# Handing out row gathers by a queue, and taking one more row block of a sparse product over edge lists

## The chip, the cores and the metric

The kernel runs on one NeuronCore of a Trainium2 chip. The metric is the device time of one execution in microseconds, and its median over runs. The engines are called by the names that the profile uses: PE (matrix products) with PEld (its weight loads), DVE (VectorE), ACT (ScalarE), POOL (GpSimd, which also issues the indirect gathers) and SP (which issues the big loads).

## The reference, cut to what matters

Four graph layers share one sparse 4096 x 4096 matrix `adj`; each is a residual with a layer norm. The change lies in layer 1, which multiplies by `adj` three times:

```python
def cheb_conv(x, L, W, b):
    Tx0 = x
    out = Tx0 @ W[0]
    Tx1 = L @ x
    out = out + Tx1 @ W[1]
    for k in range(2, W.shape[0]):
        Tx2 = 2.0 * (L @ Tx1) - Tx0
        out = out + Tx2 @ W[k]
        Tx0, Tx1 = (Tx1, Tx2)
    return out + b
h = elu(cheb_conv(x, adj, W0, b0))     # 128 -> 256
h = elu(cheb_conv(h, adj, W1, b1))     # 256 -> 128
x = layernorm(x + h)
```

The kernel does `adj @ x` (product 1, giving `t1`), `adj @ t1` (product 2, giving `t2` and from it `h` and `v`), and then, with the second convolution factored, `adj @ v` (product 3, giving `w`) and `adj @ w` (product 4). `adj` is sparse: the kernel provides for up to 24 entries in a row apart from the diagonal. All four products are in float32.

## The kernel before, in words

**Dense products.** `propagate` (lines 723 to 737) walks over row blocks of 512 rows. For each it loads eight chunks of 512 x 512 (1 MB each, through SP, into a pool `ld` of five buffers) and does four 128x512 matrix products for each chunk. A float32 product of 128x512 shows as two records in the profile, so that a row block is 64 records. After each chunk a hook is called (`seen`); the text counts these hooks from 0 in each product, eight to a row block. Product 1 runs over the row blocks 2, 3, 0, 4, 5, 1, 6, 7, that is 64 hooks; its chunk order is `finished`, the order in which layer 0 ended its blocks, which works out as 0, 7, 5, 1, 6, 2, 3, 4. Product 2 is dense in six row blocks (48 hooks), product 3 in five.

**Edge lists.** While chunks pass by, `Lists.take` (line 1392) finds the entries of each row on DVE: for each of a chunk's four 128-row tiles one MAX8 (line 1402) and one FIND_INDEX8 (line 1403). "A take" below is one chunk: four such pairs. Where the chunk holds the diagonal, ACT first copies each tile into a single buffer `copied` (line 1399) and DVE clears the diagonal (line 1401). `Lists.build` (line 1411) turns what was found into a list for a row block, in three parts. The lists of row blocks 0, 1, 2 (`PAIRED`) also need the matrix entries in both directions; these come by 36 gathers for each block (`pairs`, line 1533, landing in `both_ways`) and are unpacked by `paired` (line 1540).

**Sparse products.** With its list known, a row block needs no chunk. For each tile of 128 rows (a "unit") POOL gathers nine times 128 rows of the vector's table in DRAM (`rows_of`, line 1549), `weigh` (line 1554) does three TENSOR_SCALAR and six SCALAR_TENSOR_TENSOR on DVE, and `product` does one 128x128 product with the identity and three with the gathered rows. The tables are written block by block by `store` (line 1564). Product 2 takes row blocks 0 and 1 in this way (eight units, `second_product`, line 1605), product 3 row blocks 0 to 2 (twelve units, `third_product`, line 1672). In product 1 all eight row blocks are dense.

**What orders the work.** The order on PE and ACT is set by a scheduler when the program is built. On DVE, what goes through `chained` (line 1385) keeps the order in which it is written; in products 2 and 3 the takes, builds and weighs are chained, while in product 1 nothing is, and the scheduler mixes takes with other work there. POOL keeps program order. Each gather is one instruction on POOL (`by_index`, line 1523) followed by `pause` (line 1567), a 128x1 multiply of a constant with itself. Gathers are written in bursts: nine for a unit, or all 36 of a list, at one hook. In product 1 the 36 gathers for list 0 are written nine at a time, once in a row block, each time behind a pause that reads a column of the last finished `t1` block (line 765).

```python
def by_index(self, out, of, index):
    tc.keep_in_program_order(nc.gpsimd.indirect_dma_start(out, None, of, bass.IndirectOffsetOnAxis(ap=index, axis=0)))
    tc.keep_in_program_order(self.pause())
```

**After layer 1's third product** `sparse_layers` (line 1734) does product 4, six dense row blocks with two sparse ones, and then layers 2 and 3 over the lists.

Of the kernel before, what the change touches and what calls it, by code (L numbers as in the profile page):

```python
# [11 lines left out]
F32 = mybir.dt.float32  # L12
# [9 lines left out]
P = 128  # L22
# [18 lines left out]
LAST = [0, 1]  # L41
FAR = [4, 5, 6, 7]
EARLY = 7
NONE = -1e30
# [3 lines left out]
def adj_resnorm_d4(ctx: ExitStack, tc: tile.TileContext, x_in, xT_in, adj, adjT, pairs, diag_in, w0g, w0gT, a0, w1a, b1a,  # L48
# [633 lines left out]
    def network(usual):  # L682

        with ExitStack() as whole:
# [3 lines left out]
            with ExitStack() as first, ExitStack() as l1h_pool:  # L688
# [66 lines left out]

                made = lists.build(0) if usual else None
                done = []

                def beside_first(ib, n, c, a):
                    if 0 < c < FAR[0] or ib in LAST and c in FAR:  # L760
                        lists.take(ib, c, a)
                    if (len(done), n) in ((1, 0), (1, 4), (2, 0)):
                        next(made)
                    if len(done) > 2 and n == 3:
                        tc.keep_in_program_order(lists.pause(t1[:, done[-1] * TB, 0:1]))
                        fetch(0, TB * 9 // 4)

                for ib, blk, p in propagate(lambda jt: x[:, jt, :], finished, seen=beside_first, blocks=[2, 3, 0, 4, 5, 1, 6, 7]):
                    nc.scalar.copy(t1T[:, blk], p)
                    q = transpose4(ps_tr, "ptr", lambda k: t1T[:, (ib * TB + k) * P:(ib * TB + k + 1) * P])  # L770
                    nc.vector.tensor_copy(t1[:, ib * TB:(ib + 1) * TB, :], q)
                    done.append(ib)
                    if usual:
                        lists.store(2, ib, t1)

                v = state.tile([P, NT, F], F32, name="v")
# [4 lines left out]
                def second_end(ib, t2T):  # L781
# [11 lines left out]
                    nc.scalar.copy(v[:, ib * TB:(ib + 1) * TB, :], q)  # L793
                    done[-1] = ib
                    if usual:
                        lists.store(0, ib, v)

                second = second_product(lists, l1w, pairs, t1, t1T, xT, hT, v, done, t2_of, second_end) if usual else None

# [12 lines left out]
                if usual:  # L812
                    fetch(PAIRED[-1], TB * 9)
                    lists.paired(PAIRED[-1])
                    l1s = l1h_pool.enter_context(tc.tile_pool(name="l1s", bufs=2, reuse_waits="tile"))
                    third = third_product(lists, l1s, ps_tr, ps_mm, v, w, hT, W1B, wd, h0T)
# [5 lines left out]
                for ib, blk, p in propagate(lambda jt: v[:, jt, :], beside=times_w1, seen=third, blocks=[b for b in range(NB) if not usual or b not in PAIRED]):  # L822
# [4 lines left out]
                    if usual:  # L827
                        lists.chained(r)
                        lists.store(1, ib, w)
                    ph = ps_mm.tile([P, IB], F32, name="pmm")  # L830
# [489 lines left out]
    class Lists:  # L1320
# [3 lines left out]
        def __init__(self, whole, first, layer, own_entries):  # L1324
# [5 lines left out]
            self.table_early = dram.tile([N + 1, F + H], F32, name="table_early")  # L1330
            self.tables = [dram.tile([N + 1, F], F32, name=f"rows{n}") for n in range(3)]
            self.spread = dram.tile([NB, P, TB * SLOTS], BF16, name="spread")
            self.top = state.tile([P, NT, NB, 8], F32, name="top", tag="dv")
            self.at = keep.tile([P, NT - TB, NB, 8], U16, name="at")
            self.diag = own_entries
            self.last = None
            nc.scalar.dma_start(self.diag, diag_in)
            self.source = keep.tile([P, NT, NEAR + QT], I32, name="source")
# [184 lines left out]
        def by_index(self, out, of, index):  # L1523
            tc.keep_in_program_order(nc.gpsimd.indirect_dma_start(out, None, of, bass.IndirectOffsetOnAxis(ap=index, axis=0)))  # L1524
            tc.keep_in_program_order(self.pause())

# [77 lines left out]

    def second_product(lists, pool, pairs, t1, t1T, xT, hT, v, done, t2_of, second_end):
        units = len(LAST) * TB
# [15 lines left out]

        def pull(u):
            deque(lists.rows_of(u, got[u], 2), 0)

        def weigh(u):
            here = pool.tile([P, F], F32, name="here2", bufs=1)
            lists.weigh(u, t1[:, tile_of(u), :], got[u], here, got[u][:, E:E + QT, :], True)
            made[u] = here

        def product(u):
            t, k = tile_of(u), u % TB
            if k == 0:
                sums[0] = pool.tile([P, IB], F32, name="t2T")
            p = lists.psum.tile([P, P], F32, name="u")
            nc.tensor.matmul(p, made.pop(u), ident, start=True, stop=False)
            for j in range(QT):
                nc.tensor.matmul(p, got[u][:, j, :], got[u][:, E + j, :], start=False, stop=j == QT - 1)
            t2_of(sums[0][:, k * P:(k + 1) * P], p, slice(t * P, (t + 1) * P))
            if k == TB - 1:  # L1640
                second_end(PAIRED[u // TB], sums.pop(0))

        for c, h in ((1, 0), (2, 14)):
            build = lists.build(c, True)
            for n in range(3):
                at(h + 3 * n, next, build)
        at(0, pull, 0)
        at(0, pull, 1)
        at(7, fetch, 1, TB * E)
        at(8, lists.paired, 0)  # L1650
        at(26, lists.paired, 1)
        for u, h in enumerate((9, 11, 27, 30, 33, 35, 41, 44)):
            at(h, weigh, u)
            at(h + 1, product, u)
        for u, h in ((2, 12), (3, 13), (4, 25), (5, 25), (6, 35), (7, 37)):
            at(h, pull, u)
        at(26, fetch, 2, 12)
        at(45, fetch, 2, TB * E)
        hooks = [0]

        def seen(ib, n, c, a):
            h = hooks[0]
            hooks[0] += 1
            if c in FAR:
                lists.take(ib, c, a, True)
            for f in plan.pop(h, ()):
                f()
            if h == 47:
                assert not plan and not made and not sums
        return seen  # L1670

    def third_product(lists, pool, ps_tr, ps_mm, v, w, hT, W1B, wd, h0T):
        units = len(PAIRED) * TB
        E = NEAR + QT
        got, made = {}, {}

        def pull(u):
            if u < units:
                got[u] = pool.tile([P, E, F], F32, name="got3", bufs=3)
                deque(lists.rows_of(u, got[u], 0), 0)  # L1680

        def weigh(u):
            here = pool.tile([P, F], F32, name="here3")
            hot = pool.tile([P, QT, P], F32, name="hot3")
# [3 lines left out]
        def product(u):  # L1688
# [8 lines left out]
            nc.vector.tensor_tensor(w[:, t, :], p, here, ALU.add)  # L1697
            pull(u + 2)
            if u % TB == TB - 1:
# [12 lines left out]

        build = builds()
        pull(0)
        pull(1)
        plan = {}
        for u, h in enumerate((6, 9, 11, 14, 16, 19, 22, 24, 27, 30, 32, 35)):
            plan.setdefault(h, []).append(lambda u=u: weigh(u))
            plan.setdefault(h + 1, []).append(lambda u=u: product(u))
        plan[36].append(lambda: (deque(lists.values(3), 0), deque(lists.values(4), 0)))  # L1720
        hooks = [0]

        def seen(ib, n, c, a):
# [4 lines left out]
            for f in plan.pop(h, ()):  # L1728
                f()
            if h == 39:  # L1730
                assert not plan and next(build, None) is None
        return seen

    def sparse_layers(enter, lists, w, h0T):
# [274 lines left out]
        with tc.manual_schedule(engines={mybir.EngineType.PE, mybir.EngineType.DVE, mybir.EngineType.Activation,  # L2009
# [51 lines left out]
            for u, h in enumerate((7, 10, 13, 16, 19, 22, 25, 28)):  # L2061
                plan.setdefault(h, []).append(lambda u=u: weigh(u))
                plan.setdefault(h + 1, []).append(lambda u=u: product(u))
            pulls = pull()
            known = None
# [122 lines left out]
```

## Time and profile before

| what | value |
|---|---|
| median of 11 runs | 1644.76 us (1640.62 to 1654.07) |
| the profiled execution | 1647.62 us, span 1645.8 us |
| product 1 (335.4 to 562.8 us of the span) | PE busy 227.0 of 227.4, DVE 198.2, POOL 44.0 |
| product 2 (562.8 to 800) | PE busy 229.3 of 237.2, DVE 197.3, POOL 173.6 |
| product 3 (800 to 1000) | PE busy 188.8 of 200, DVE 160.1, POOL 149.6 |
| clock granted to PE from 335 to 1000 us | 1.00 |

The span is what the profiler saw of the program; the execution's own time has 1.8 us around it. The stages are cut where PE's first product of each kind begins. A busy time is the union of the records of an engine's instructions in the stretch.

### The profile page before, as it was taken

How to read it: one execution, taken by the hardware profiler on the slowest of the kernel's cores; microseconds unless marked ns; L12 is line 12 of the kernel's file. 1: busy time of each engine (PE TensorE's matmuls, PEld its weight loads, DVE VectorE, ACT ScalarE, POOL GpSimd, SP SyncE). 2: the span in 40 equal slices, each digit the busy share in tenths (PEclk: the TensorE clock that was granted, in tenths of full speed). 3: DMA queues.
4: the chain of work that ended last, by engine and by line, in shares of the span. 5: the costliest groups of instructions: out<-in, count | busy, mean ns of one | idle time of the engine just before them, and what ended most of it. 6: DMA issues, size and time to landing. Idle time of an engine off the chain costs nothing.

```text
span 1645.8 us, 16500 instructions
## 1 busy us (share of the span) xinstructions
PE 1473.4 (90%) x4740; PEld 712.4 (43%) x4744; DVE 1140.1 (69%) x3209; ACT 387.9 (24%) x698; POOL 837.0 (51%) x1336
## 2 busy tenths in 40 slices
PE   6899999999999999999999999799925798879885
PEld 3344444544444444454444454444413344444444
DVE  5887655789887897988699950355426855666776
ACT  5775540010000011121200000123213111122234
POOL 0000000000242088848486888888686688888841
PEclk9899999999999999999999999899967788889998
DMA  9867776479798886867587888799865577678773
GB/s 381 338 257 301 255 259 239 177 260 326 300 329 308 308 283 210 292 203 274 176 296 250 288 285 291 239 311 285 285 160 149 176 237 246 225 229 291 233 191 101
DMA packets 111199, 421.47 MB, mean 256 GB/s; under 512 B 21685, under 2 KB 48314, under 8 KB 71290
## 3 DMA queue, kind: packets, MB, share of 16 engines
q1 hardware_dynamic: 59984, 360.01, 60.8%
q0 software_dynamic: 22656, 36.17, 9.0%
q10 hardware_dynamic: 28458, 24.14, 5.0%
q8 instruction: 39, 0.64, 0.2%
q14 instruction: 62, 0.51, 0.1%
HBM read 404.39 MB, written 15.86 MB: 255 GB/s over the span
## 4 chain that ended last, share of the span: by engine, by line
PE 47%; DVE 25%; POOL 12%; DMA 8%; issue 5%; ACT 2%; DVEq 0%; ACTq 0%; POOLq 0%
PE pacc L731 16%; PE pacc L424 12%; PE pp L2076 6%; POOL got L1846 5%; DMA got<-table,source 4%; PE pp L1957 3%; DVE at L1403 3%; DVE top L1402 3%; POOL got L1524 2%; POOL idle L1569 2%; DMA got<-rows,source 2%; DVE gw L1882 1%; DVE here L1562 1%; DVE acc L1970 1%; POOL value L1524 1%
## 5 line engine op out<-in xcount | busy, mean ns | idle before, releaser
L1846 POOL DMA_INDIRECT got<-table,source x267 | 255.5, 957 | 64.8 <-issue 58.8
L1957 PE MATMUL pp<-chunk,xT 128*128 128x512 f32 x496 | 244.4, 634 | 1.2 <-ACT xT L1928 0.7
L731 PE MATMUL pacc<-chunk,x 128*128 128x512 f32 x512 | 222.7, 593 | 0.0
L1524 POOL DMA_INDIRECT got<-rows,source x180 | 183.5, 1020 | 67.4 <-issue 37.0
L424 PE MATMUL pacc<-chunk,hw 128*128 128x512 f32 x408 | 189.2, 608 | 0.8 <-DVE hw L467 0.7
L1360 POOL IOTA i<- 128x384 int32 (+3 forms) x4 | 0.9, 237 | 346.6 <-PE pden L412 329.5
L2076 PE MATMUL pp<-chunk,w 128*128 128x512 f32 x384 | 173.0, 600 | 0.0
L731 PE MATMUL pacc<-chunk,t 128*128 128x512 f32 x384 | 170.3, 593 | 0.0
L731 PEld LDWEIGHTS pacc<-chunk,x 128*128 128x128 f32 x512 | 96.1, 190 | 114.6 <-issue 114.6
L731 PE MATMUL pacc<-chunk,v 128*128 128x512 f32 x320 | 144.5, 597 | 0.0
L1402 DVE MAX8 top<-chunk 128x8 f32<-128x512 f32 x196 | 128.5, 677 | 11.8 <-DMA chunk<-in_adjT 11.8
L1957 PEld LDWEIGHTS pp<-chunk,xT 128*128 128x128 f32 x496 | 94.3, 203 | 91.3 <-issue 85.5
L1403 DVE FIND_INDEX8 at<-top,chunk 128x8 uint16<-128x512 f32 x196 | 133.1, 684 | 0.0
L1569 POOL TENSOR_TENSOR idle<-idle 128x1 f32<-128x1 f32 x508 | 114.2, 225 | 8.8
L1524 POOL DMA_INDIRECT both_ways<-in_pairs,both_at x108 | 106.6, 987 | 17.4 <-issue 17.1
L424 PEld LDWEIGHTS pacc<-chunk,hw 128*128 128x128 f32 x408 | 75.1, 192 | 92.3 <-issue 87.0
L731 PEld LDWEIGHTS pacc<-chunk,t 128*128 128x128 f32 x384 | 71.1, 190 | 80.7 <-issue 80.7
L2076 PEld LDWEIGHTS pp<-chunk,w 128*128 128x128 f32 x384 | 71.6, 193 | 79.1 <-issue 78.3
L396 ACT ACTIVATE junk<-chunk 128x2048 fp8e4<-128x2048 f32 x51 | 97.4, 1910 | 28.5 <-DMA chunk<-in_adjT 27.8
L330 DVE TENSOR_SCALAR pos<-chunk 128x2048 bf16<-128x2048 f32 x66 | 80.2, 1220 | 32.4 <-DMA chunk<-in_adjT 30.3
L1889 PE MATMUL u<-gw,into 128*128 128x132 f32 x192 | 33.3, 317 | 71.3 <-DVE gw L1882 71.2
L731 PEld LDWEIGHTS pacc<-chunk,v 128*128 128x128 f32 x320 | 58.3, 190 | 65.5 <-issue 65.5
(433 smaller groups left out, 2063.5 us busy)
## 6 DMA issues: line engine op xcount, KB each, us to landing
chunk<-in_adjT SPq DMA_DIRECT2D x326, 1024.0 KB, 6.1
keep<-in_adjT SPq DMA_DIRECT2D x13, 1024.0 KB, 8.4
spread<-spread ACTq DMA_DIRECT2D x16, 384.0 KB, 4.5
got<-table,source POOLq DMA_INDIRECT x267
chunk<-in_adjT ACTq DMA_DIRECT2D x4, 1024.0 KB, 8.4
got<-rows,source POOLq DMA_INDIRECT x180
table<-rows ACTq DMA_DIRECT2D x8, 264.0 KB, 10.0
xT<-in_xT ACTq DMA_DIRECT2D x8, 256.0 KB, 7.9
```

Of the source, the lines that this page charges most:

```text
L330: r = nc.vector.tensor_scalar(pos, a, 0.0, None, op0=ALU.is_gt)
L396: nc.scalar.activation(junk, a, AF.Relu, scale=-1.0, accum_out=bad[:, n:n + 1], saturate=False)
L424: in_order(nc.tensor.matmul(p, hw[:, j * TB + k, :], a[:, k, :], start=first and k == 0, stop=last and k == TB - 1))
L731: nc.tensor.matmul(p, stationary(c * TB + k), a[:, k, :], start=n == 0 and k == 0, stop=n == NB - 1 and k == TB - 1)
L1402: pin(nc.vector.max(self.top[:, t, ib, :], row))
L1403: pin(nc.vector.max_index(self.at[:, t - TB, ib, :], self.top[:, t, ib, :], row))
L1524: tc.keep_in_program_order(nc.gpsimd.indirect_dma_start(out, None, of, bass.IndirectOffsetOnAxis(ap=index, axis=0)))
L1569: return nc.gpsimd.tensor_tensor(self.idle[:, 0:1], of, self.idle[:, 1:2], ALU.mult)
L1846: nc.gpsimd.indirect_dma_start(got[t][:, j, :], None, table, bass.IndirectOffsetOnAxis(ap=lists.source[:, t, j:j + 1], axis=0))
L1889: nc.tensor.matmul(so, into[:, j, :], gw[:, j, :], start=j == 0, stop=False)
L1957: nc.tensor.matmul(p, y[:, t0 + k, :], a[:, ib % (TB // n), k, :], start=k == 0, stop=k == n - 1)
L2076: nc.tensor.matmul(p, w[:, c * TB + k, :], a[:, k, :], start=n == 0 and k == 0, stop=n == NB - 1 and k == TB - 1)
```

## The change

Row block 0 (`SPARE`) of product 1 is no longer dense: `propagate` runs over 2, 3, 4, 5, 1, 6, 7 (56 hooks), and a new function `first_product` makes row block 0 out of four sparse units that gather from a fourth table, to which `x` is stored. The chunks of row block 0 other than its first are still needed by the takes: chunks 1 to 3 are loaded aside at hooks 13, 27 and 47 of product 1, chunks 4 to 7 at hooks 15, 22, 38 and 46 of product 2. All takes of product 1, the build of list 0 and the copies that end a `t1` block are now chained on DVE.

Gathers are no longer written in bursts. `ask` puts a generator of gathers into a queue with the first hook at which it may run; `feed` is called at each hook and takes 2.7, 3.4 or 3.5 gathers a hook from the queue (products 1, 2 and 3); `finish` takes all that is left where a result is needed. Each gather's pause now reads `lists.fresh`, a column of the last result that came from PE (a `t1`, `v` or `w` block, or a sparse unit's result). In product 3 a unit's gathers are asked for three units ahead, not two. From product 4 on, the pauses are as they were.

```diff
+SPARE = 0
@@ layer 1, product 1
-                made = lists.build(0) if usual else None
-                def beside_first(ib, n, c, a):
-                    if 0 < c < FAR[0] or ib in LAST and c in FAR:
-                        lists.take(ib, c, a)
-                    if (len(done), n) in ((1, 0), (1, 4), (2, 0)):
-                        next(made)
-                    if len(done) > 2 and n == 3:
-                        tc.keep_in_program_order(lists.pause(t1[:, done[-1] * TB, 0:1]))
-                        fetch(0, TB * 9 // 4)
-                for ib, blk, p in propagate(..., blocks=[2, 3, 0, 4, 5, 1, 6, 7]):
+                def first_end(ib):
                     q = transpose4(...)
-                    nc.vector.tensor_copy(t1[:, ib * TB:(ib + 1) * TB, :], q)
+                    r = nc.vector.tensor_copy(t1[:, ib * TB:(ib + 1) * TB, :], q)
                     done.append(ib)
                     if usual:
+                        lists.chained(r)
+                        lists.fresh = t1[:, ib * TB, 0:1]
                         lists.store(2, ib, t1)
+                for ib, blk, p in propagate(..., blocks=[2, 3, 4, 5, 1, 6, 7] if usual else range(NB)):
@@ Lists
         def by_index(self, out, of, index):
...
-            tc.keep_in_program_order(self.pause())
+            tc.keep_in_program_order(self.pause(self.fresh))
+        def ask(self, hook, rows):
+            self.queue.append((hook, rows))
+            return rows
+        def feed(self, hook, rate):
+            self.credit += rate
+            while self.credit >= 1 and self.queue and self.queue[0][0] <= hook:
+                if next(self.queue[0][1], self) is self:
+                    self.queue.popleft()
+                else:
+                    self.credit -= 1
+            self.credit = min(self.credit, rate)
+        def finish(self, rows=None):
+            while self.queue and any(rows is None or r is rows for _, r in self.queue):
+                deque(self.queue.popleft()[1], 0)
@@ new
+    def first_product(...):
...
+        build = lists.build(SPARE, True)
+        for h in (2, 6, 9):
+            at(h, next, build)
+        for ib in range(NB):
+            at(8, lists.store, 3, ib, x)
+        lists.ask(10, pairs[SPARE])
+        for u in range(TB):
+            lists.ask(11, rows[u])
+        at(30, known)
+        for u, h in enumerate((32, 36, 39, 43)):
+            at(h, weigh, u)
+            at(h + 1, product, u)
+        for h, c in ((13, 1), (27, 2), (47, 3)):
+            at(h, take_spare, c)
...
+            if SPARE < c < FAR[0] or ib in LAST and c in FAR:
+                lists.take(ib, c, a, True)
...
+            lists.feed(h, 2.7)
@@ second_product (the order of the gathers is that of before)
+        for h, what in ((2, 0), (2, 1), (7, (1, TB * E)), (12, 2), (14, 3), (25, 4), (25, 5), (26, (2, 12)), (35, 6), (37, 7), (45, (2, TB * E))):
...
+        for h, c in zip((15, 22, 38, 46), FAR):
+            at(h, lambda c=c: lists.take(SPARE, c, spare_chunk(c), True))
+            lists.fresh = sums[0][:, k * P:k * P + 1]
+            lists.feed(h, 3.4)
@@ third_product
-            pull(u + 2)
+            lists.fresh = w[:, t, 0:1]
+            pull(u + 3)
-        plan[36].append(lambda: (deque(lists.values(3), 0), deque(lists.values(4), 0)))
+        plan[34] = [lambda: (lists.ask(34, lists.values(3)), lists.ask(34, lists.values(4)))]
+            lists.feed(h, 3.5)
```

`known` finishes the gathers for list 0 and calls `paired(0)`. Shortened argument lists are marked by dots.

## The prediction, on record before the result was known

> **What bounds it now.** I read the stages first (busy time of each engine in stretches of one row block), then the chain that ended last, then who waited for whom, then the order of time on DVE and POOL. In the stages a row gives the stretch, its length, and busy us of PE, PEld, DVE, ACT and POOL; behind them stand the granted clock, the DMA share and GB/s.
>
> ```profile
> 392.00:420.00 28.00, 28.00 (x80) 12.58 (x79) 28.00 (x78) 1.20 (x2) 0.00 (x0) 1.00 0.78 267
> 449.00:477.00 28.00, 28.00 (x70) 12.53 (x69) 19.01 (x44) 0.59 (x1) 10.79 (x19) 1.00 0.96 350
> 477.00:506.00 29.00, 29.00 (x72) 12.90 (x71) 29.00 (x72) 3.06 (x5) 10.79 (x19) 1.00 0.83 295
> 772.00:800.00 28.00, 27.88 (x84) 13.64 (x83) 15.01 (x35) 6.52 (x11) 17.73 (x30) 1.00 0.56 197
> ```
>
> All of product 1 (335.4 to 562.8) looks like the first three: PE without a gap, at full clock. The reader should also see DVE: in row blocks 0 and 1, where seven chunks are taken and not three, it is full as well. Over product 1, PE is busy 227.0 of 227.4 us and DVE 198.2; over product 2, 229.3 and 197.3 of 237.2. The chain says the same: whole row blocks of PE, and in product 2 pieces of DVE.
>
> ```profile
> 452.55 27.47 PE pacc L731 x64
> ...
> 568.99 4.00 DMA rows<-t
> 573.19 0.71 issue
> 573.89 0.97 POOL hT L1524
> ```
>
> So PE bounds product 1 and DVE stands close behind it. PE's waits from product 1 to product 3 are small, and what they name is DVE:
>
> ```profile
> PE pmm L786 <- DVE t2T L779: 5.2, 4, 3.1
> PE u L1478 <- DVE spread L1318: 3.2, 4, 1.4
> ```
>
> **The dense block that goes.** Its 64 records are 27.5 us of PE (the chain's row). A sparse unit is eight records; in product 2 one ran from 609.58 to 610.47, 0.89 us, so four cost 3.6. Transposes stay. PE needs 227.0 - 27.5 + 3.6 = 203.1 us. That is -23.9 if nothing else ends later.
>
> **DVE in product 1.** This decides, because what was mixed is now chained. Unchained, takes are interleaved two rows at a time; chained, each row waits for its own maximum; with the diagonal, a chained take also waits for ACT's copy of each tile:
>
> ```profile
> 410.40 1.27 DVE L1402 MAX8 top<-chunk 128x8 f32<-128x512 f32 x2
> ```
> ```profile
> 645.15 0.69 DVE L1402 MAX8 top<-copied 128x8 f32<-128x512 f32 x1
> ...
> 647.38 0.29 DVE L1401 SCALAR_TENSOR_TENSOR copied<-ident,copied 128x128 f32<-128x128 f32 x1 [0.74 <-ACT copied L1399]
> 647.71 0.69 DVE L1402 MAX8 top<-copied 128x8 f32<-128x512 f32 x1
> ...
> 696.73 0.87 DVE L1559 TENSOR_SCALAR hT<-iota,into_column,back 128x128 f32<-128x128 f32 x3
> 697.52 2.28 DVE L1562 SCALAR_TENSOR_TENSOR here<-hT,back,here 128x128 f32<-128x128 f32 x6
> 699.72 0.69 DVE L1402 MAX8 top<-chunk 128x8 f32<-128x512 f32 x1
> ```
>
> Interleaved, the next pair begins at 412.91: 2.51 us for two rows, 5.0 a take. Chained, rows start 1.39 apart (562.71, 564.11), 5.56 a take. With the diagonal they start 2.56 apart, 10.2 a take; mixed in, such a row added 1.45 to its neighbours (pairs 3.96 apart at 487 to 499), 5.8 a take.
>
> - Takes before: 32, of them 3 on the diagonal: 29 x 5.0 + 3 x 5.8 = 162.7. After: 28 (four far chunks go to product 2): 25 x 5.56 + 3 x 10.2 = 169.6. Fewer takes, +6.9 us.
> - Four weighs at 2.99 (696.73 to 699.72): +12.0. `paired` for list 0 moves here: +0.3.
> - Of the 198.2, 7.2 us (555.47 to 562.71) were product 2's first build part, run early because DVE had room.
>
> DVE's own work in product 1 is then 198.2 - 7.2 + 0.7 (the last `t1` copy) + 19.2 = 210.9 us, more than PE's 203.1. It has 2.7 us at the start that it still waits (W1B). The last `t1` block would be copied at 335.4 + 210.9 + 2.7 = 549.0; it was copied at 568.3. Both ends: 541 (203.1 and the transposes, if DVE's lag is hidden) and 561 (another 12 us, as much as DVE waited for chunks in products 1 to 3).
>
> **DVE in product 2.** Before, DVE had done product 2's first build part and first take when it came to 568.87. After, those 12.8 us follow 549.0, so it reaches the same point at 561.8, 7.1 early. Then come four more takes, 22.2, less `paired` 0.3. From 562.8 to 800 DVE stood idle 237.2 - 197.3 = 39.9 us. How much of that can be filled, the trace does not show. A DVE that comes late no longer waits for `elu` (11.0), for a weigh's ACT copy (4.6) or for t2T's products (4.5); it still waits for ACT's `copied` (10.3) and for list sums. I take the 20.1 of the first three as filled; ends 10 and 35. Product 2 then ends 22.2 - 0.3 - 20.1 - 7.1 = -5.3 us. PE alone could end earlier, but the last t2T is chained behind the takes, and `v`'s last store releases product 3's gathers, so I count DVE's end.
>
> **Gathers and their pauses.** A gather with its pause takes 1.35 us wherever nothing holds it:
>
> ```profile
> 575.24 0.97 POOL hT L1524
> 576.59 0.97 POOL hT L1524
> ```
>
> Product 1 now has 72, 97 us, fed over hooks 10 to 37 (28 x 3.43 = 96). Unit 0's nine end by hook 29, its weigh is at 32; unit 3's end near 40, its weigh is at 43. They are in time. In product 2 the 144 gathers are 194 us in 237. A pause there now waits for a `v` block, and `v` is ready some 18 us after its row block's last product (628.5; stored at 646.8). Some 20 gathers are fed before hook 8; they end at 573.9 + 27 = 601, and the next pause waits for the first `v` block, whose products end at 608: 7 us, and a few more after the next block. Units 2 and 3 are gathered by 680 and not 670, and their weighs start at 696. So 0; the ends are 0 and +6, if later units lose the same 10 us against less room. In product 3 the third unit asked ahead finds no buffer: there are three, and the third comes free when the product that asks has run. Product 3's gathers ran one after another from 884 to 987, so the earlier hook for `values` frees nothing: 0, ends -8 (what product 4's first unit waited for the queue) and +4.
>
> By the trace a gather is slower while DVE runs two-input instructions: 1.24 us at 819 to 825 beside `same`, 0.97 beside takes. The Trainium skill states this (GPSIMD Engine Reference, Key points): POOL shares its SBUF interfaces with VectorE and contends with instructions of two SBUF inputs. That speaks against putting weighs beside gathers. It would lengthen some five gathers in product 1, an estimate of 2 us on a queue with room; the sum stays as it is.
>
> **DMA.** Per row block: eight chunks, in three of seven a ninth, in one also eight stores of `x` (2.1 MB). That worst block moves 11.5 MB, at the 350 GB/s of 449 to 477 some 33 us against 28. Eighteen row gathers took 23.7% of 24 us of all DMA engines, 0.32 us each, 11 us for 36. Five buffers let a load start four chunks (13.7 us) ahead and land in 5 to 8, which covers about 6. I take 0; the ends are 0 and +5.
>
> **Sum.** -5.3 + 0 + 0 = -5.3: the profiled 1647.62 would be 1642.3, and the median of the runs, 2.9 below it, 1644.76 - 5.3 = 1639.5.
>
> **Rivals.**
> 1. DVE does not bind: its lag stays inside the buffers and its idle time takes the rest. PE's -23.9 stays but for about 2: 1623. For it: in row blocks 0 and 1 DVE was full and PE did not stop once. Against: the sum of 210.9.
> 2. Slower: DVE's lag reaches PE through the chunk buffers. The place is product 1's hooks 32 to 43: row block 1 asks DVE for 6 x 5.56 + 10.2 + 3 x 2.99 = 52.5 us in some 30 of PE, a lag of 22 where the buffers hide about 7; the chunks behind stop PE, and product 2 begins full of takes. If only 7 of product 2's 39.9 idle us can be filled, it ends 22.2 - 0.3 - 7 - 7.1 = +7.8, and with 4 more for the stores and gathers in that place +12: 1657. It decides if less than 15 us are filled. For it: before, DVE was late for t2T four times with less to do.
> 3. The pauses do what they say and that costs: POOL comes too late for product 2's later units, +6 on top of filled time: 1651. Against: the walk above.
>
> A PE that stops for long loses clock too: in the slices 1200 to 1300 us PE is half busy and the clock 0.69, from 335 to 1000 it is 1.00 with waits of at most 3.1. The skill's rule (TensorE: Matmul & The Clock Gate, the HAM clock gate) is that an idle window of some 3.4 us halves the clock. By that rule rival 2's stalls would each cost up to 1.7 us more, an estimate; the sum by the rows leaves it out.
>
> **Chances.** About 0.3% (4.9 us) is what a measurement of this kernel can tell from no change, so faster means below 1639.8 and slower above 1649.7. The forecast, by itself 1631 to 1646, has 0.34: 0.20 below the bound, 0.14 within. Rival 1 has 0.20, all faster. Rival 2 has 0.36: 0.34 slower, 0.02 same. Rival 3 has 0.10: 0.06 slower, 0.04 same. Faster 0.40, same 0.20, slower 0.40. The range takes in nearly all of the forecast, most of rivals 2 and 3 and the edge of rival 1: 1625 to 1660.
>
> **What would show it.** Product 1 ending between 541 and 551 with DVE above 95% busy in its last five row blocks; its first PE waits for chunks, in row block 1; the last `t1` copy near 549; no DVE wait for `got` in products 1 and 2; DVE's idle time in product 2 halved; product 3's gathers starting some 5 us earlier. DVE waiting for gathers in products 1 or 2 would make rival 3 right, PE waiting for chunks by more than 10 us rival 2. The forecast is wrong if DVE's waits cannot be filled, or if the scheduler places the units so late on PE that the chain has no say.

## The result, and the profile after

The changed kernel took 1689.45 us (median of 8 runs, 1688.07 to 1695.34), the kernel before 1645.35 us (31 runs). The ratio is 1.0274, 95% interval 1.0255 to 1.0292: 44 us slower, and outside the range that was forecast (1625 to 1660). The profiled execution took 1697.34 us, its span 1695.1.

Where the time went is read from the stages, cut as before where PE's first product of each kind begins: product 1, product 2, product 3 of the kernel after (columns as in the prediction: length, busy us of PE, PEld, DVE, ACT, POOL, granted clock, DMA share, GB/s).

```profile
335.00:559.80 224.80, 213.35 (x556) 96.48 (x554) 194.69 (x512) 16.05 (x32) 85.88 (x147) 0.98 0.82 295
559.80:817.00 257.20, 237.62 (x676) 111.99 (x675) 229.62 (x611) 43.42 (x74) 151.32 (x251) 0.95 0.71 249
817.00:1046.50 229.50, 197.14 (x599) 94.61 (x597) 159.55 (x574) 15.76 (x31) 169.49 (x266) 0.94 0.70 232
```

| stage (us, profiled) | before | after | constant pauses | dense block 0, reading pauses | dense block 0, constant pauses |
|---|---|---|---|---|---|
| product 1 | 227.4 | 224.8 | 218.1 | 227.2 | 227.2 |
| product 2 | 237.2 | 257.2 | 255.4 | 237.0 | 239.8 |
| product 3 | 199.2 | 229.5 | 199.7 | 228.1 | 198.8 |
| all behind it | 646.6 | 648.6 | 651.4 | 645.1 | 643.4 |

Product 1 hardly gained, product 2 lost 20 us and product 3 lost 30. (The last three columns are experiments below. The row behind product 3 scatters by 8 us in no order, so single profiles are compared by the stages ahead of it.)

The chain that ended last has shifted the same way (before, PE held 47% of it and DVE 25%):

```profile
PE 34%; DVE 33%; POOL 15%; DMA 7%; issue 6%; ACT 4%; ACTq 0%; DVEq 0%; POOLq 0%
```

The waits between 335 and 1046.5 say what ended last. Of the kernel after, PE and DVE first, then POOL:

```profile
PE ptr L1791 <- DVE hot L1577: 16.0, 6, 4.9
PE pacc L732 <- DMA chunk<-in_adjT: 11.9, 4, 5.5
PE u L1455 <- DVE count L1317: 10.6, 3, 9.2
DVE here L1580 <- DMA got<-rows,source: 30.9, 19, 3.4
DVE value L1564 <- DMA both_ways<-in_pairs,both_at: 19.1, 1, 19.1
POOL idle L1587 <- ACT v L791: 69.8, 4, 32.3
POOL idle L1587 <- DVE w L1794: 28.7, 1, 28.7
```

Before, PE did not wait for a chunk once in these products. Now there are two stories. The chunk waits belong to products 1 and 2. The rest belongs to product 3: POOL's pauses (`idle`) stood for `v` and `w`, DVE then stood for gathers, and PE for DVE. The longest hold, in order of time on POOL and then on DVE:

```profile
776.88 0.98 POOL L1525 DMA_INDIRECT both_ways<-in_pairs,both_at  x1 [0.15 <-issue]
810.19 0.19 POOL L1587 TENSOR_TENSOR idle<-v,idle 128x1 f32<-128x1 f32 x1 [32.33 <-ACT v L791]
810.87 1.06 POOL L1525 DMA_INDIRECT both_ways<-in_pairs,both_at  x1 [0.49 <-issue]
```
```profile
818.23 0.17 DVE L1563 CAST number<-source 128x36 f32<-128x36 int32 x1
...
843.75 0.18 DVE L1564 COPY value<-both_ways 128x36 f32<-128x36 f32 x1 [19.07 <-DMA both_ways<-in_pairs,both_at]
...
845.14 0.23 DVE L1317 CAST count<-degree 128x4 bf16<-128x4 f32 x1
```

Before, POOL had run the same 24 gathers without a hold and was done with them 9 us before DVE came for what they bring (POOL, then DVE):

```profile
758.68 0.97 POOL L1524 DMA_INDIRECT both_ways<-in_pairs,both_at  x1 [0.15 <-issue]
...
790.90 0.97 POOL L1524 DMA_INDIRECT both_ways<-in_pairs,both_at  x1 [0.15 <-issue]
```
```profile
801.11 0.18 DVE L1546 COPY value<-both_ways 128x36 f32<-128x36 f32 x1
```

The reader is to see one queue stop another. In the kernel after, at 776.9, POOL was some 30 us ahead of PE and had 24 gathers left for list 2. The pause behind the first of them was written three hooks before the end of product 2 and reads the `v` block of the sparse row block 1, which is finished at that hook and is there at 810. The other 23 gathers, 1.35 us each, end at 842. What waits for them is `paired` for list 2 (`value`), and that stands first in product 3's DVE chain: all builds and weighs of that product are behind it, so DVE lost 19.1 us and PE waited 9.2 for the next build's `count`.

### The profile page after: what moved, and what is told of

It reads as the page before. It is cut to its first block, busy times and chain, and to the rows that moved or that the text cites. A ratio compares the mean times of both kernels' runs of the same rounds, so it can differ in the third digit from the quotient of the medians.

```text
span 1695.1 us, 16590 instructions
## 1 busy us (share of the span) xinstructions
PE 1478.1 (87%) x4708; PEld 715.0 (42%) x4712; DVE 1168.6 (69%) x3245; ACT 389.0 (23%) x705; POOL 882.2 (52%) x1403
## 4 chain that ended last, share of the span: by engine, by line
PE 34%; DVE 33%; POOL 15%; DMA 7%; issue 6%; ACT 4%; ACTq 0%; DVEq 0%; POOLq 0%
PE pacc L425 12%; DVE at L1404 7%; PE pp L2056 6%; DVE top L1403 5%; POOL got L1525 4%; PE pacc L732 4%; PE pp L2177 4%; DMA got<-table,source 3%; POOL got L1945 3%; POOL idle L1587 3%; DVE here L1580 2%; POOL both_ways L1525 2%; DVE spread L1317 2%; POOL value L1525 1%; DVE same L1317 1%
## 5 line engine op out<-in xcount | busy, mean ns | idle before, releaser
L732 PE MATMUL pacc<-chunk,x 128*128 128x512 f32 x448 | 202.0, 606 | 2.3 <-DMA chunk<-in_adjT 2.1
L732 PE MATMUL pacc<-chunk,t 128*128 128x512 f32 x384 | 180.2, 620 | 9.8 <-DMA chunk<-in_adjT 9.8
L732 PE MATMUL pacc<-chunk,v 128*128 128x512 f32 x320 | 149.4, 611 | 0.0
L1403 DVE MAX8 top<-chunk 128x8 f32<-128x512 f32 x196 | 132.7, 677 | 1.4 <-DMA chunk<-in_adjT 1.4
L732 PEld LDWEIGHTS pacc<-chunk,x 128*128 128x128 f32 x448 | 84.7, 194 | 103.5 <-issue 95.5
L1525 POOL DMA_INDIRECT hT<-rows,source x72 | 71.8, 997 | 93.5 <-DVE there L1317 82.7
L397 ACT ACTIVATE junk<-chunk 128x2048 fp8e4<-128x2048 f32 x51 | 97.4, 1909 | 29.3 <-DMA chunk<-in_adjT 28.8
L1580 DVE SCALAR_TENSOR_TENSOR here<-got,back,here 128x128 f32<-128x128 f32 x120 | 42.5, 354 | 80.5 <-DMA got<-rows,source 77.9
```

The lines of the kernel that those rows point to most:

```text
L397: nc.scalar.activation(junk, a, AF.Relu, scale=-1.0, accum_out=bad[:, n:n + 1], saturate=False)
L732: nc.tensor.matmul(p, stationary(c * TB + k), a[:, k, :], start=n == 0 and k == 0, stop=n == NB - 1 and k == TB - 1)
L1403: pin(nc.vector.max(self.top[:, t, ib, :], row))
L1580: pin(nc.vector.scalar_tensor_tensor(here, got[:, j, 0:F], self.back[:, u, j:j + 1], here, op0=ALU.mult, op1=ALU.add))
```

## The experiments

Times are medians; ratios are to the kernel before in the same set of runs, with 95% intervals. The kernel before took 1644 to 1648 in all sets but one.

**Pauses and block 0, one by one.** Four kernels: constant pauses in the changed kernel, product 1 dense as before with and without reading pauses, and the kernel before with reading pauses.

```diff
-            tc.keep_in_program_order(self.pause(self.fresh))
+            tc.keep_in_program_order(self.pause())
```

> The changed kernel (1689) with pauses that read a constant, as before the change; queue and sparse block 0 stay. Theory A, held pauses: POOL stood 98 us at pauses that waited for a v or w block, so the gathers for list 2 and for product 3's units came late and DVE waited for them; without that, product 3 falls from 227 us back to about 197 and product 2 loses a few us too: 1650 to 1660. Theory B, full DVE: the chained takes and weighs of block 0 make DVE late, and pauses wait only because the blocks are late: 1680 to 1690. Theory C, spacing: the queue hands gathers out too late whatever the pause reads: 1680 to 1690.

Measured: 1659.21, ratio 1.0072 (1.0054 to 1.0091), as theory A has it: product 3 is back at 199.7 us.

The next kernel takes product 1 from the kernel before (and sets `lists.fresh` there):

```diff
@@ second_product
-        for h, c in zip((15, 22, 38, 46), FAR):
-            at(h, lambda c=c: lists.take(SPARE, c, spare_chunk(c), True))
+        at(8, lists.paired, 0)
```

> The changed kernel with product 1 as before the change (all eight blocks dense, takes not chained, no takes of block 0 in product 2), but queue and reading pauses in products 2 and 3. Theory A (held pauses): product 1 as before, products 2 and 3 still lose what the pauses hold: 1665 to 1685. Theory B (full DVE): 1640 to 1650. Theory C (spacing): 1665 to 1685.

Measured: 1675.99, ratio 1.0184 (1.0165 to 1.0204). POOL's holds are the same without any sparse work in product 1:

```profile
793.39 0.19 POOL L1591 TENSOR_TENSOR idle<-v,idle 128x1 f32<-128x1 f32 x1 [32.57 <-ACT v L795]
...
880.99 0.19 POOL L1591 TENSOR_TENSOR idle<-w,idle 128x1 f32<-128x1 f32 x1 [29.56 <-DVE w L1797]
```

The same with constant pauses:

> As the run with product 1 dense, and pauses that read a constant: of the change only the queue is left. Theory A (held pauses) and theory B (full DVE): as before the change, 1640 to 1650. Theory C (spacing): 1665 to 1685.

Measured: 1646.70, ratio 1.0001 (0.9983 to 1.0019). The queue by itself costs and gains nothing.

In the kernel before, with `lists.fresh` set where the change sets it:

```diff
-            tc.keep_in_program_order(self.pause())
+            tc.keep_in_program_order(self.pause(self.fresh))
```

> The kernel before, with one thing of the change: each pause of products 1 to 3 reads a column of the last result from PE. Bursts and the dense block 0 stay. Theory A (held pauses): POOL is held at v and w blocks as in the changed kernel, 1660 to 1685. Theories B (full DVE) and C (spacing): 1640 to 1650.

Measured: 1682.65, ratio 1.0220 (1.0200 to 1.0239). With bursts the reading pauses cost 37 us; with the queue (1675.99) 30.

What follows: the parts add up. Queue +1.2 (1646.7 against 1645.5), sparse block 0 +12.5 (1659.2 against 1646.7), reading pauses +30.2 (1689.4 against 1659.2) or, with a dense block 0, +29.3. Theory B and theory C fall as the cause of the 30 us; B is left as the cause of the 12.5, which the runs on block 0 below go into.

**Which pauses.** First the result before the last is read, in place of the last (`results` is the list of all of them):

```diff
-            tc.keep_in_program_order(self.pause(self.fresh))
+            tc.keep_in_program_order(self.pause(self.results[-2] if len(self.results) > 1 else None))
```

> The changed kernel (1689); each pause reads the result before the last one and not the last. Theory A (held pauses): what costs is the wait for a result whose work has not run yet; the one before it is mostly there, so most of the 30 us between reading pauses (1689) and constant ones (1659) comes back: 1660 to 1672. Rival: the reading itself costs (another operand, another semaphore on POOL), whatever is read: 1685 to 1690.

Measured: 1686.83, ratio 1.0236 (1.0197 to 1.0275), which looks like the rival. The profile says no: the result before the last was not there either, and POOL stood for it at the same place.

```profile
796.99 0.19 POOL L1587 TENSOR_TENSOR idle<-t2T,idle 128x1 f32<-128x1 f32 x1 [26.46 <-DVE t2T L777]
```

So this run tells nothing of whether reading by itself costs. The next three do, since in each some pauses read a result long there or a constant:

```diff
@@ product 2 (e2)
-                        lists.fresh = v[:, ib * TB, 0:1]
-            lists.fresh = sums[0][:, k * P:k * P + 1]
@@ product 3 (e3)
-                        lists.fresh = w[:, ib * TB, 0:1]
-            lists.fresh = w[:, t, 0:1]
@@ gathers of matrix entries only (e11)
-        def by_index(self, out, of, index):
+        def by_index(self, out, of, index, read=True):
...
-            tc.keep_in_program_order(self.pause(self.fresh))
+            tc.keep_in_program_order(self.pause(self.fresh if read else None))
-                    yield self.by_index(self.both[:, u, j, :], flat, self.both_at[:, u, j:j + 1])
+                    yield self.by_index(self.both[:, u, j, :], flat, self.both_at[:, u, j:j + 1], False)
```

> The changed kernel (1689); the pauses of product 2 go on reading the last t1 block, long there, and not v or t2T; those of products 1 and 3 as changed. Theory G (the wait at the end of product 2 costs most: 24 gathers for list 2 stand behind a pause that waits 32 us for the last v block, and the unpacking of list 2, first in product 3's DVE chain, waits 19 us for them): 1665 to 1672. Rival H (the waits for w in product 3 cost most, since POOL has 108 gathers left there): 1682 to 1689.

> The changed kernel (1689); the pauses of product 3 go on reading the last v block and not w; those of products 1 and 2 as changed. Theory G (end of product 2): the 29 us hold for w is gone, but POOL starts product 3 as late as before, so 5 to 12 us come back: 1677 to 1684. Rival H (the waits for w cost most): 1660 to 1668.

> The changed kernel (1689); only the pauses behind gathers of matrix entries for lists 0 to 2 read a constant, those behind row gathers read as changed. Theory G (the 24 gathers for list 2 at the end of product 2 are what is late): the same as with all of product 2 constant, 1665 to 1673. Rival I (the held row gathers cost, not those of the list): 1680 to 1689.

Measured: 1669.77 (ratio 1.0164, 1.0134 to 1.0195), 1682.74 (1.0226, 1.0190 to 1.0261) and 1671.43 (1.0179, 1.0143 to 1.0215). All three are where theory G has them. Freeing the gathers of the lists alone (e11 frees those for lists 0 and 1 too) gives back what freeing all of product 2 gives, and in both runs DVE no longer waits for `both_ways` in product 3: the hold on list 2 is worth 18 to 20 us. The holds for `w` are worth the rest: with no `v` or `t2T` read in product 2 (e2), product 3 still took 209.5 us and not 199.7. Taking the holds for `w` away alone (e3) gives 7 and leaves product 3 at 223.5, so the two overlap. Each run keeps the other one's wait, e2 the first line and e3 the second:

```profile
POOL idle L1587 <- DVE w L1794: 17.5, 1, 17.5
```
```profile
DVE value L1564 <- DMA both_ways<-in_pairs,both_at: 18.9, 1, 18.9
```

Reading by itself costs nothing that shows: product 2 took 256.6 us in e2, whose pauses read a `t1` block long there, and 255.4 with constant pauses. In the kernel after, the hold for `w` looks like this, POOL first, then PE at the end of product 3:

```profile
868.59 0.98 POOL L1525 DMA_INDIRECT got<-rows,source  x1 [0.15 <-issue]
898.30 0.19 POOL L1587 TENSOR_TENSOR idle<-w,idle 128x1 f32<-128x1 f32 x1 [28.73 <-DVE w L1794]
...
1036.83 1.01 POOL L1525 DMA_INDIRECT got<-rows,source  x1 [0.15 <-issue]
```
```profile
1005.54 0.94 PE L1791 MATMUL ptr<-got,hot 128*128 128x128 f32 x4 [3.58 <-DVE hot L1577]
...
1018.07 1.19 PE L1791 MATMUL ptr<-got,hot 128*128 128x128 f32 x4 [4.66 <-DVE hot L1577]
...
1029.33 0.80 PE L1791 MATMUL ptr<-got,hot 128*128 128x128 f32 x2 [4.89 <-DVE hot L1577]
```

At 868.6 POOL had issued 18 of product 3's 108 row gathers. The other 90 need 90 x 1.35 = 121 us, so from 898 on POOL could not be done before 1020, and it ended at 1038; in the last units DVE and PE wait for it.

**Block 0 on DVE.** All from the kernel with constant pauses (1659). First the takes of passing chunks are not chained:

```diff
-                lists.take(ib, c, a, True)
+                lists.take(ib, c, a)
```

> The changed kernel with constant pauses (1659), the takes of product 1's passing chunks not chained, so that the scheduler mixes them as before the change. Theory D (the chain of DVE in product 1 is the bound): by the rows 25 takes at 5.0 and 3 at 5.8 in place of 5.56 and 10.2, 27 us less for DVE; product 1 is then bound by PE and some 10 us come back: 1642 to 1652. Rival E (the loads aside and PE's chunk waits are the bound, not DVE): within 3 us of 1659. Rival F: without a chain the scheduler places weighs late and PE waits for them: above 1662.

Measured: 1647.86, ratio 1.0000 (0.9983 to 1.0016), 0.72% better than chained. Product 1 is 211.5 us long and not 218.1, and DVE is busy 180.6 us in it and not 194.6 (products 1 and 2 of this run):

```profile
335.09:546.56 211.47, 205.19 (x547) 94.24 (x546) 180.61 (x518) 16.05 (x32) 86.80 (x147) 0.99 0.88 320
546.56:799.55 252.99, 234.79 (x683) 110.96 (x682) 226.69 (x604) 43.45 (x74) 175.46 (x288) 0.99 0.70 248
```

Theory D; E and F fall.

Then the diagonal rows are copied in turn to two pieces of `hT` that product 1 leaves free:

```diff
-                    row = self.spare.tile([P, IB], F32, name="copied", bufs=1, tag="elu_r")
+                    row = rows[k % 2] if rows else self.spare.tile([P, IB], F32, name="copied", bufs=1, tag="elu_r")
-                lists.take(ib, c, a, True)
+                lists.take(ib, c, a, True, [hT[:, hh, 7 * IB:8 * IB] for hh in range(2)])
```

> The changed kernel with constant pauses (1659); in product 1 the copies of diagonal rows go to two buffers in turn, so that DVE need not wait for ACT's copy at 9 of 12 rows (0.74 each, 6.7 us in the changed kernel's profile). Theory D (DVE's chain is the bound): 5 to 7 us less, 1652 to 1655. Rival E (loads): within 2 us of 1659.

Measured: 1654.91, ratio 1.0057 (1.0034 to 1.0079), which is 0.15% or 2.5 us better, within the two intervals. The copies' waits are gone, but those for the transposes grew (2.2 to 6.5 us), and product 1 is only 2.3 shorter. The direction fits theory D, the size does not settle it.

Then four takes are left out (what they would have found is set to zero, so the lists lack entries; the loads stay):

```diff
-            at(h, lambda c=c: lists.take(SPARE, c, spare_chunk(c), True))
+            at(h, lambda c=c: spare_chunk(c))
```

> The changed kernel with constant pauses (1659); the four takes of block 0's far chunks in product 2 are left out (their four loads stay), so that lists 4 to 7 lack block 0's entries and the output is not the reference. Theory D (DVE is the bound in product 2): 22.2 us of DVE work less, of which the change's 18 us longer product 2 gives back 9 to 18: 1641 to 1651. Rival E (the four more loads stop PE in product 2): within 3 us of 1659.

Measured: 1646.41, ratio 0.9991 (0.9972 to 1.0011): 13 us better. Product 2 with constant pauses, and then without the four takes:

```profile
553.40:808.80 255.40, 235.81 (x675) 111.27 (x674) 228.93 (x610) 43.45 (x74) 175.78 (x288) 0.96 0.72 250
```
```profile
555.30:798.90 243.60, 231.45 (x676) 109.80 (x675) 208.58 (x564) 43.35 (x74) 175.79 (x288) 0.98 0.75 263
```

DVE has 20.4 us less to do and the stage is 11.8 shorter. The four loads stayed, so they are not what it was; rival E falls. PE's waits for chunks in product 2 fell with the takes, from 10.1 to 3.2 us. Mixing the takes of product 1 and leaving these four out each give back about all of the 12.5. That sum is a net one: dropping the dense block also saves PE's time, and the kernel of the next experiment, which mixes these takes and moves the four in place of leaving them out, takes less time than the kernel before the change.

**A version that beats both.** When the takes of product 1 are mixed, DVE has 30.9 us left beside PE there (211.5 - 180.6). So, on top of constant pauses and mixed takes, block 0's far chunks are taken in product 1 and not in product 2:

```diff
-        for h, c in ((13, 1), (27, 2), (47, 3)):
+        for h, c in ((13, 1), (19, 4), (27, 2), (31, 6), (38, 5), (47, 3), (51, 7)):
-        for h, c in zip((15, 22, 38, 46), FAR):
-            at(h, lambda c=c: lists.take(SPARE, c, spare_chunk(c), True))
```

> Constant pauses, mixed takes in product 1 (the kernel that took 1648), and block 0's four far chunks taken in product 1 (hooks 19, 31, 38, 51) and not in product 2. Theory D (DVE's work is the bound where it has no room): product 1 has some 30 us of idle DVE beside PE, product 2 has none; product 2 falls from 249 us to about 238 and product 1 grows by 0 to 8: 1637 to 1645. Rival J (product 1 is full as well, and the loads aside stop PE there): 1646 to 1655.

Measured: 1639.16, ratio 0.9972 (0.9952 to 0.9992), as theory D has it; product 2 is 242.1 us long and not 253.0, product 1 214.1 and not 211.5. Two variants of it came to a chip on which the kernel before itself took 1821 us. Both were slower than that (ratios 1.0127 and 1.0163), with DVE and PE standing up to 49 us for what the trace only calls remote or issue; these two runs are not used.

One has two of the four in product 2, the other has block 0's own takes not chained:

```diff
@@ e14
+        for h, c in ((13, 1), (27, 2), (47, 3), (20, 4), (37, 6)):
+        for h, c in ((22, 5), (46, 7)):
@@ e15
-            lists.take(SPARE, c, spare_chunk(c), True)
+            lists.take(SPARE, c, spare_chunk(c))
```

> As the run with all four far chunks of block 0 taken in product 1 (1639), but two of them (5 and 7) taken in product 2 at hooks 22 and 46. Theory D (each take in product 2 costs what product 2's DVE has no room for): half way between four takes there (1648) and none (1639): 1642 to 1646. Rival K (only the order in product 1 matters, not where the four takes stand): within 2 us of either end.

> As the run with all four far chunks of block 0 taken in product 1 (1639), with block 0's own seven takes mixed in as well, not chained. Theory D (DVE's work is what binds): seven takes at 5.0 in place of 5.56, 4 us less for DVE, of which PE at 203 of 214 us can use some: 1634 to 1639. Rival L (a mixed take of a chunk loaded aside is placed late, keeps its buffer and stops PE): 1640 to 1650.

All three were run again on one other chip:

> The kernel with constant pauses, mixed takes and all four far chunks of block 0 taken in product 1, beside the next two on one chip: 4 to 7 us faster than the kernel before, as in its first run, 1637 to 1642 where that takes 1644. If its first result was chance: no difference from before.

Measured: 1638.30, ratio 0.9956 (0.9938 to 0.9975). It is faster than both kernels, by 0.3 to 0.4% of the one before.

> Two of the four far chunks (5 and 7) taken in product 2 at hooks 22 and 46, the other two in product 1. On the chip of the earlier try the kernel before itself took 1821, so that it told nothing of this. Theory D (each take in product 2 costs what product 2's DVE has no room for): half way between four takes there (1648) and none (1639): 1642 to 1646. Rival K (only the order in product 1 matters): within 2 us of either end.

Measured: 1640.69, ratio 0.9970 (0.9954 to 0.9986). The time misses the 1642 to 1646 of theory D. Rival K (within 2 us of an end) has it by the 1639 that it was written for, and just misses it by the 1638.30 of this set. By ratios half way between four takes (1.0000) and none (0.9956) is 0.9978, which this interval holds, so the time settles neither. The stage, one profile each, tells more: product 2 is 253.0 us with four takes, 244.3 with two, 242.0 with none. Where the takes stand matters, but not all cost the same: the two that were left (hooks 22 and 46) cost 2, the two that went (15 and 38) 9.

> All four far chunks in product 1, block 0's own seven takes mixed in as well, not chained. Theory D (DVE's work is what binds): 4 us less for DVE, of which PE can use some: 1634 to 1639. Rival L (a mixed take of a chunk loaded aside is placed late, keeps its buffer and stops PE): 1640 to 1650.

Measured: 1643.86, ratio 0.9986 (0.9965 to 1.0006), in the range of rival L. The profile is of the slowest of its ten executions (1654.13), with a product 1 of 227.8 us. In it DVE waits 9.0 us for list 0's matrix entries, and PE once for a buffer that a take still holds:

```profile
DVE value L1564 <- DMA both_ways<-in_pairs,both_at: 9.0, 1, 9.0
...
PE pacc L732 <- DVE at L1404: 3.7, 1, 3.7
```

So the wait of rival L is there; that it makes the median's 5.6 us over the first of the three is not shown.

## Why the prediction was wrong, step by step

The forecast was -5.3 us, and +44.1 came, 49.4 more. The pauses are 30 of it and DVE's terms for products 1 and 2 are 14, as the paragraphs below work out. The rest, some 5, is less than single profiles scatter behind product 3 (8 us); where it arises stays open.

**The pauses: the step that failed.** The prediction counted them at nothing in product 2, and in product 3 it gave no term to a pause at all. For product 2 itself the nought held: with a dense block 0 it took 237.0 us with reading pauses and 239.8 with constant ones, though POOL was held there as well. What failed is the walk of the queue. It went as far as units 2 and 3, with some 10 us of holds, and stopped; POOL was held 69.8 us behind `v` blocks, 10.5, 9.2, 17.8 and then 32.3. It left out the 24 gathers for list 2 at the end of product 2, whose consumer is not in product 2 but first in product 3's DVE chain. The rows for it were there: 24 x 1.35 = 32 us of POOL's time behind a `v` block that comes with the end of the stage, against a `paired` that DVE came to at 801.1, 1 us into product 3. Rival 3 named the mechanism, gave it the wrong place (product 2's later units) and +6 us; it is worth 30.

**Product 3's third unit asked ahead**, counted at nothing: right by itself. With constant pauses product 3 is 199.7 us against 199.2. But the same line of thought, that POOL runs one gather after another from 884 to 987 without slack, should have been carried on: POOL has no room there for a hold of 29 us.

**DVE in product 1.** The sum put the last `t1` copy at 549.0. With constant pauses it came at 555.9, in the kernel after at 562.7. What the sum missed above all is that a chain also waits at its head. With constant pauses, DVE's waits in product 1 were:

```profile
DVE copied L1402 <- ACT copied L1400: 6.7, 9, 0.7
DVE top L1403 <- DMA chunk<-in_adjT: 5.5, 1, 5.5
DVE wd L745 <- DMA W1B<-in_w1b: 2.3, 1, 2.3
DVE t L761 <- PE ptr L156: 2.2, 1, 2.2
```

The first and third were in the sum. A chunk that is late (5.5) and transposes that are late (2.2) were not, and 7.7 is about what is missing (6.9). Without the last three waits the 220.6 us to that copy are 210.6, against the 210.9 of the sum. That fit is luck in part: the 210.9 held 2.4 us of list 1's build that had run at 542 before and now came behind the copy. (Two figures of the working are off by 0.3: the 32 takes before come to 162.4 and not 162.7, and DVE waited 4.3 and not 4.6 for a weigh's ACT copy. Neither matters.) With mixed takes DVE waited longer for chunks (14.3) and for transposes (6.6), but had 14.0 us less to do, and product 1 was shorter all the same. Why the kernel after lost another 7 us in product 1 is not settled: W1B came later there (DVE waited 7.1), and the profiles of seven kernels that do the same work in product 1 end it between 553 and 560.

**DVE in product 2.** The sum had three terms, and all can be read from DVE's second take of the stage to its end, before and then with constant pauses:

```profile
568.87:799.98 231.11, 223.16 (x667) 107.37 (x666) 191.30 (x504) 42.99 (x73) 173.58 (x288) 1.00 0.72 247
571.71:808.81 237.10, 217.51 (x629) 103.02 (x628) 211.77 (x548) 42.86 (x73) 172.60 (x284) 0.96 0.71 248
```

DVE was to reach that take 7.1 early and reached it 2.8 late (571.71 against 568.87): 6.9 of these 9.9 are the late end of product 1, and 3.0 are the stretch from the last copy on, which took 15.8 and not 12.8 (the copy itself and those 2.4 us of the build). The takes less `paired` were to add 21.9 and DVE was busy 20.5 longer. Of its idle time 20.1 was to be filled, and 14.5 was (39.8 left before, 25.3 now). 2.8 + 20.5 - 14.5 = +8.8 and not -5.3, and product 2 did end at 808.8 against 800.0. That it closes proves nothing, since busy and idle time make up the stretch; it shows which terms were off: the lead by 9.9, the filled time by 5.6. The filled part is just below the 15 from which rival 2 was to decide. That the sparse block's +12.5 is that rival's +12 is luck in part: rival 2 had 7 us filled and a DVE 7.1 early.

**DMA**, counted at nothing: right as far as the runs show. Leaving four takes out and keeping their loads gave the time back, and took 6.9 of PE's 10.1 us of chunk waits in product 2 with it. So most of these waits came from DVE's takes; that it was by the buffers they held is the likely way and is not shown row by row.

**The signs it named beforehand.** "PE waiting for chunks >10 us" for rival 2: 11.9. "DVE waiting for gathers in products 1 or 2" for rival 3: none there; the wait came 8 us into product 3, one stage behind the place that was watched. The forecast's own signs failed: product 1 ended at 559.8 and not between 541 and 551, and product 3's gathers began at 842.5 and not some 5 us before the 814.5 of the kernel before. The chances had 0.40 on slower, shared out between two rivals as if only one could come. Both came, in different stages, and added up.

## What to carry to other kernels

A wait put into an in-order queue ties everything behind it to the hook at which it was written; where that queue runs ahead of the engine it now waits for, the lead is lost. So walk the queue to its last entry and then to the first consumer in the next stage, and ask what is chained behind that consumer. And before moving work between stages, ask which stage has idle time on the engine that gets it: the same four takes cost 11 us in product 2 and 3 to 4 in product 1 (single profiles).

## What the runs showed of the hardware

A stop of PE cost more than its own length. These are two stops in product 2 of the kernel after, in order of time on PE:

```profile
649.29 3.78 PE L732 MATMUL pacc<-chunk,t 128*128 128x512 f32 x4 [4.18 <-DMA chunk<-in_adjT]
652.86 3.17 PE L784 MATMUL pmm<-t2T,W1A 128*128 128x512 f32 x4
655.87 1.88 PE L732 MATMUL pacc<-chunk,t 128*128 128x512 f32 x4
...
686.95 13.55 PE L732 MATMUL pacc<-chunk,t 128*128 128x512 f32 x24 [5.49 <-DMA chunk<-in_adjT]
```

At the pace of before (64 records in 27.47 us, 0.43 each) the eight records from 649.29 to 655.87 take 3.4 us and took 6.6; the 24 from 686.95 take 10.3 and took 13.55. Each of the two cost 3.2 us on top of its own 4.2 and 5.5. The granted clock of the first and the last of these groups, behind length and busy times:

```profile
649.29:653.10 3.81, 3.81 (x5) 1.74 (x6) 1.15 (x2) 0.00 (x0) 3.32 (x7) 0.50 0.99 296
686.95:700.50 13.55, 13.55 (x24) 5.56 (x24) 13.21 (x31) 0.00 (x0) 6.02 (x11) 0.78 0.73 256
```

The clock was 0.50 after a wait of 4.2 us. The rule of the Trainium skill that the prediction weighed (TensorE: Matmul & The Clock Gate, the HAM clock gate: an idle window halves the clock) agrees with that; the loss was about twice the 1.7 us that was estimated from it. With constant pauses the 384 records of chunk products in product 2 kept PE busy 179.2 us and not 170.3, at a clock of 0.96 over the stage and not 1.00: 8.9 us that go with the lower clock, beside 10.1 us of waits for chunks.

```profile
L731 PE MATMUL pacc<-chunk,t 128*128 128x512 f32 x384 | 170.3, 593 | 0.0
```
```profile
L732 PE MATMUL pacc<-chunk,t 128*128 128x512 f32 x384 | 179.2, 618 | 10.1 <-DMA chunk<-in_adjT 10.1
```
